# A two-layer graph attention kernel: the range check's PSUM bank, two x tiles turned at other places, and the selection copies on other engines

## The chip, the cores and the metric

The kernel runs on one core of one Trainium2 chip. The metric is the device time of one execution in microseconds (us), the median of several runs. Beside it stands one profiled execution, whose trace gives the start and the duration of every instruction. All times inside the kernel are from the start of that execution's span.

A core has five engines that run their own instruction streams and meet at semaphores: TensorE (PE in the profile; its weight loads are shown apart as PEld), VectorE (DVE), ScalarE (ACT), GpSimd (POOL) and SyncE (SP), which here only issues DMAs. TensorE writes into PSUM, of which this kernel uses eight banks of 128 x 512 fp32.

## The reference

The reference is a two-layer graph attention network with a residual and a layer norm. There are 512 nodes with 768 features and 8192 + 8192 + 512 = 16896 edges (`src`, `dst`), sorted by `dst`.

```python
def gat_layer(x, W, a_s, a_d, b, edge_index, concat):
    h = (x @ W).reshape(n, H, C)
    alpha_s = jnp.einsum('nhc,hc->nh', h, a_s)
    alpha_d = jnp.einsum('nhc,hc->nh', h, a_d)
    e = jax.nn.leaky_relu(alpha_s[src] + alpha_d[dst], NEG_SLOPE)
    m = jax.ops.segment_max(e, dst, num_segments=n)
    e = jnp.exp(e - m[dst])
    denom = jax.ops.segment_sum(e, dst, num_segments=n)
    alpha = e / (denom[dst] + EPS)
    msg = h[src] * alpha[:, :, None]
    out = jax.ops.segment_sum(msg, dst, num_segments=n)
    return out.reshape(n, H * C) + b
h = elu(gat_layer(x, W1, a_src1, a_dst1, b1, ...))     # 8 heads of 768
out = gat_layer(h, W2, a_src2, a_dst2, b2, ...)        # 1 head of 768
return layernorm(x + out)
```

The result depends on the edges only through how often each pair (dst, src) occurs. So the kernel counts the pairs into a 512 x 512 matrix `cnt` and replaces gathers and segment sums by dense matmuls with that matrix.

## The kernel before

**Two passes.** `gat_pass` is traced twice. The first pass (with a `flag`) assumes that each chunk of 128 sorted edges has its destinations in one or two known blocks of 32 nodes. A range check counts how many destinations lie in their block; `flag` is the number of edges minus that count. If it isn't zero, the second, general pass runs; with these inputs it doesn't. All instructions are issued in the order in which the program is written: `manual_schedule` moves nothing, so the order of the source is the order of each engine's stream.

**The loads.** SP issues, in this order: the indices `dst` and `src`, the left halves of W1 for head 0 (two quarters, k chunks 0 to 2 and 3 to 5), x tile 3, the right halves of W1, x tiles 0 and 1, b1, the attention vectors, then the weights of head 1. ScalarE's queue issues x tile 2 at the very start. An x tile is 128 rows of x.

**The opening, lines 148 to 227.** TensorE first runs matmuls on a tile of zeros (`keep_warm`, line 154), whose result in the bank of pool `bc` no one reads. In the meantime GpSimd builds an identity `ident`. From it come the selection columns `pick` (line 212): for each run of chunks with the same blocks, a copy of a few columns of `ident`, repeated once or twice. VectorE makes the runs of the first half of the chunks (16 copies), GpSimd those of the second half (16 copies, between its memsets of `base`, line 215). VectorE converts the indices (`idx_f`, line 217). Two matmuls (line 221) with `pick` and two transposes (line 223) put the indices edge by edge into the PSUM tile `psi`, and VectorE reads it twice: `rel` (line 225), the destination relative to its block, and `idx` (line 227), the sources.

**The x tiles.** `turn_x(t)` (line 353) transposes the six 128 x 128 pieces of an x tile on TensorE (line 357) into two banks of pool `mm`, and ScalarE copies them into `xT` (line 358).

**The counting stage, lines 425 to 528.** There are 132 chunks of 128 edges in nine batches of 16, 16, 13, 16, 13, 16, 13, 16 and 13. For each batch VectorE builds a one-hot of the sources for each chunk (`os`, line 456, 32 rotating buffers) and, in four quarters, one-hots of the destinations (`odw`, line 441). TensorE multiplies the two (line 473, 32 columns of weights), adding into the count tile `cps[t]` of each 128 destinations. Between the counts of two batches the program places pieces ("items") of head 0's projection: an item is three matmuls of line 382 (six rows in the trace, as each fp32 matmul is two), for one x tile, one half of the columns and one half of the contraction. The first items need, in this order, x tile 2 with the first W1 quarter, x tile 2 with the second, then x tile 3 with each. `turns` says before which item another `turn_x` is put. The count of a batch comes after its items. After item 15 come steps of the next head's projection (line 269).

**PSUM.** Pool `mm` has five banks, `tr` two and `bc` one. A tile of a pool takes the pool's banks in rotation, and has to wait until the earlier tile in that bank has been read. In the counting stage `tr` holds, in order, `psi`, `pst`, `cps[0]`, `cps[1]`, `cps[3]` and the tile of `spread(0)`; `bc` holds the warm-up's tile and then `cps[2]`.

**The range check.** `inside` (lines 446 to 450, VectorE, beside batch 0) leaves the number of edges in range per partition in `found`. In batch 1, ahead of the count, TensorE adds the partitions up into `pst` (line 524). In batch 3, ahead of that batch's one-hots, VectorE turns `pst` into `flag` (line 501); in batch 4 the engines load it into registers. `xsums[:1]` (`xS`, line 249), a difference of two parts of `xT` with x tiles 2 and 3, stands behind batch 2's one-hots on VectorE, ahead of the flag.

After the counting stage come, for each of the eight heads, softmax weights, aggregation, and a second projection in a scheme with seven products in place of eight (lines 559 to 918), and at the end the residual with the layer norm.

Of the kernel before, what the change touches and what calls it, by code (L numbers as in the profile page):

```python
# [8 lines left out]
F32 = mybir.dt.float32  # L9
# [14 lines left out]
def kernel(tc: tile.TileContext, *args):  # L24


    with ExitStack() as ctx:
        flags = ctx.enter_context(tc.tile_pool(name="flags", bufs=1))
        ctx.enter_context(tc.manual_schedule())
        flag = flags.tile([1, 1], I32, name="flag")  # L30
        again = gat_pass(tc, flag, *args)
        with tc.If(again != 0):
            gat_pass(tc, None, *args)
# [3 lines left out]
def gat_pass(  # L37
# [16 lines left out]
    nc = tc.nc  # L54
    P = 128
    N, D = x.shape
# [3 lines left out]
    DC = D // P  # L60
    HALF = D // 2
    EC = E // P
    EH = EC // 2
# [7 lines left out]
    keep = ctx.enter_context(tc.tile_pool(name="keep", bufs=1))  # L71
# [6 lines left out]
    mm = ctx.enter_context(tc.tile_pool(name="mm", bufs=5, space=bass.MemoryType.PSUM))  # L78
    tr = ctx.enter_context(tc.tile_pool(name="tr", bufs=2, space=bass.MemoryType.PSUM))
    bc = ctx.enter_context(tc.tile_pool(name="bc", bufs=1, space=bass.MemoryType.PSUM))  # L80
# [52 lines left out]
    x_sb = hpool.tile([P, NT, D], F32, name="hs")  # L133
# [18 lines left out]
    def keep_warm(n):  # L152
        for _ in range(n):
            nc.tensor.matmul(idle, zeros[:, :P], zeros, start=True, stop=True)  # L154

    keep_warm(13)
    nodes = ohp.tile([P, N], F16, name="nodes")
    nc.gpsimd.iota(nodes, pattern=[[1, N]], base=0, channel_multiplier=0,
                   allow_small_or_imprecise_dtypes=True)
    ident = const.tile([P, P], F32, name="ident")  # L160
# [9 lines left out]
                                op=ALU.add)  # L170
    far = const.tile([P, 1], F32, name="far")
    nc.vector.memset(far, -NO_EDGE)


    general = flag is None
    idx_f = ohp.tile([EH, 2, 2, P], F32, name="idx_f")
    if general:
        nc.vector.tensor_copy(idx_f, idx_i)
        idx = ohp.tile([P, 2, EC], F32, name="idx")
        psi = tr.tile([P, 512], F32, name="tr")  # L180
        for j in range(2):
            for r in range(2):
                nc.tensor.transpose(psi[:, (2 * j + r) * EH:(2 * j + r + 1) * EH], idx_f[:, j, r, :],
                                    ident[:EH, :EH])
        nc.vector.tensor_copy(idx, psi[:, :2 * EC].rearrange("p (j c) -> p j c", j=2))
    else:

        B, SLACK = 32, 10  # L190
        blocks = []
        for c in range(EC):
            m = (c + 0.5) * P * N / E
            b = int(m // B)
            lo, hi = b - (m - b * B < SLACK), b + ((b + 1) * B - m < SLACK)
            blocks.append(range(max(lo, 0), min(hi, N // B - 1) + 1))
        at = [0]
        for b in blocks:
            at.append(at[-1] + len(b))
        NB = at[EC]  # L200
        assert NB + EC <= 512 and max(map(len, blocks)) <= 2


        pick = ohp.tile([EH, NB], F32, name="pick")
        base = ohp.tile([P, NB], F32, name="base")
        lo = 0
        while lo < EC:
            hi, k = lo + 1, len(blocks[lo])
            while hi % EH and blocks[hi] == blocks[lo]:
                hi += 1  # L210
            engine = nc.vector if lo < EH else nc.gpsimd
            engine.tensor_copy(pick[:, at[lo]:at[hi]].rearrange("p (c k) -> p c k", k=k),
                               ident[:EH, lo % EH:(hi - 1) % EH + 1].unsqueeze(2).to_broadcast([EH, hi - lo, k]))
            for j, b in enumerate(blocks[lo]):
                nc.gpsimd.memset(base[:, at[lo]:at[hi]].rearrange("p (c k) -> p c k", k=k)[:, :, j], float(b * B))
            lo = hi
        nc.vector.tensor_copy(idx_f, idx_i)
        psi = tr.tile([P, 512], F32, name="tr")
        for r in range(2):
            cols = slice(at[r * EH], at[(r + 1) * EH])  # L220
            nc.tensor.matmul(psi[:, cols], idx_f[:, 0, r, :], pick[:, cols], start=True, stop=True)
        for r in range(2):
            nc.tensor.transpose(psi[:, NB + r * EH:NB + (r + 1) * EH], idx_f[:, 1, r, :], ident[:EH, :EH])
        rel = ohp.tile([P, NB], F16, name="rel")
        nc.vector.tensor_tensor(rel, psi[:, :NB], base, op=ALU.subtract)
        idx = ohp.tile([P, EC], F32, name="idx")
        nc.vector.tensor_copy(idx, psi[:, NB:NB + EC])

    cnt = keep.tile([P, NT, N], F32, name="cnt")
    absent = keep.tile([P, NT, N], BF16, name="absent")  # L230
    xT = keep.tile([P, DC, N], F32, name="xT")
    xS = keep.tile([P, 3, HK, HN], F32, name="xS")
    scr = keep.tile([P, D], BF16, name="scr")
    V = keep.tile([P, DC, 2], F32, name="V")
# [114 lines left out]
            else:  # L349
                nc.sync.dma_start(sums1[name], part)  # L350


    def turn_x(t):
        for ks in (range(4), range(4, DC)):
            ps = mm.tile([P, 512], F32, name="mm")
            for j, k in enumerate(ks):
                nc.tensor.transpose(ps[:, j * P:(j + 1) * P], x_sb[:, t, k * P:(k + 1) * P], ident)  # L357
            nc.scalar.copy(xT[:, ks.start:ks.stop, t * P:(t + 1) * P],  # L358
                           ps[:, :len(ks) * P].rearrange("p (k n) -> p k n", n=P))

    b1T = const.tile([P, H * DC], F32, name="b1T")
    nb1T = const.tile([P, H * DC], F32, name="nb1T")
# [62 lines left out]
    if not general:  # L425
# [53 lines left out]
                done += 1  # L479


        turns = {2: 3, 5: 0, 9: 1}
        keep_warm(1)
        turn_x(2)
        keep_warm(2)
        found = const.tile([P, 1], F32, name="found")
        pst = tr.tile([P, 512], F32, name="tr")
        wholes = len(items)

        extra = {0: [inside], 2: xsums[:1], 4: [lambda: logits(0, HS[0], 2)],  # L490
# [5 lines left out]
        for n, batch in enumerate(batches):  # L496
# [9 lines left out]
            while pos < want:  # L506
                if pos == wholes:
                    pairs = projection(1, XA, B1)
                    items += [lambda p=p: (p[0](), p[1]()) for p in pairs[:4]]
                if pos in turns:  # L510
                    turn_x(turns[pos])
                items[pos]()
                pos += 1
# [15 lines left out]
    else:  # L529
        for t in range(NT):  # L530
            ps = mm.tile([P, 512], F32, name="mm")
            for c in range(EC):
                o1 = ohp.tile([P, P], BF16, name="od", bufs=4)
                o2 = ohp.tile([P, N], BF16, name="os", bufs=32)
                nc.vector.tensor_scalar(o1, nodes[:, t * P:(t + 1) * P], idx[:, 0, c:c + 1], None,
                                        op0=ALU.is_equal)
                nc.vector.tensor_scalar(o2, nodes, idx[:, 1, c:c + 1], None, op0=ALU.is_equal)
                nc.tensor.matmul(ps[:, :N], o1, o2, start=c == 0, stop=c == EC - 1)
            counted(t, ps)
            turn_x(t)  # L540
# [385 lines left out]
    for t in range(NT):  # L926
# [4 lines left out]
        for g, cols in enumerate(parts):  # L931
            ps = mm.tile([P, 512], F32, name="mm")
# [49 lines left out]
```

## Time and profile before

| what | us |
|---|---|
| median of 3 runs | 659.54 |
| lowest and highest run | 658.95, 659.97 |
| the profiled execution's own time | 660.72 |
| its span, first to last instruction | 658.9 |
| busy time of TensorE / VectorE / ScalarE / GpSimd in the span | 646.7 / 508.1 / 248.6 / 51.8 |
| mean granted TensorE clock | 0.994 |

The span in 40 slices of some 16.5 us: each digit is the busy share in tenths, PEclk the granted TensorE clock.

```profile
PE   8899999999999999999999999999999999999995
...
DVE  6998789977779587867779587767776589866785
...
PEclk9899999999999999999999999999999999999998
```

TensorE is busy all through, but for the first two slices and the last. Outside of them VectorE has room. A row such as `25.44 0.83 PE tr L473 x12` in the chain of waits means: from 25.44 us on, for 0.83 us, the chain of work that ended last lay on twelve TensorE instructions of line 473 that write a tile of pool `tr`. In the waits, `PE tr L473 <- DVE flag L501` means that TensorE's instruction of line 473 was held by VectorE's instruction of line 501. A busy time on TensorE is start to modelled end, so a row can be longer than the distance to the next row.

### The profile page before, as it was taken

The page shows a single profiled execution, that of the slowest core. Times are in us where ns is not written, and L with a number is a line of the kernel's source. Part 1 is how long each engine was busy: PE and PEld are TensorE (multiplying, and loading weights), DVE is VectorE, ACT ScalarE, POOL GpSimd, SP SyncE. Part 2 cuts the span into 40 slices and gives each one's busy share as a digit, 9 for nine tenths or more (in the row PEclk, how much of TensorE's full clock was granted, in tenths as well). Part 3 has the DMA queues.
Part 4 walks back from the last instruction along what each step waited for, and adds up shares of the span by engine and source line. Part 5 has one row for each costly group of instructions (what it writes and reads, how often), then busy time and mean ns, then how long its engine had stood idle before and what let it go on. Part 6 is the DMA issues. An engine that isn't in the chain of part 4 may idle for free.

```text
span 658.9 us, 7043 instructions
## 1 busy us (share of the span) xinstructions
PE 646.7 (98%) x2365; PEld 401.0 (61%) x2365; DVE 508.1 (77%) x1116; ACT 248.6 (38%) x417; POOL 51.8 (8%) x106
## 2 busy tenths in 40 slices
PE   8899999999999999999999999999999999999995
PEld 4455577556865577556855577556755545644553
DVE  6998789977779587867779587767776589866785
ACT  2122646350645125350735135530726033333440
POOL 3230011000100110010000110010000100000000
PEclk9899999999999999999999999999999999999998
DMA  8984189177803982087704791197606864000122
GB/s 314 308 143 85 32 258 283 45 218 154 239 0 66 250 227 73 17 236 186 177 1 97 217 258 42 28 253 200 135 1 159 210 210 132 25 0 1 29 59 77
DMA packets 74154, 89.70 MB, mean 136 GB/s; under 512 B 36678, under 2 KB 58750, under 8 KB 74110
## 3 DMA queue, kind: packets, MB, share of 16 engines
q1 hardware_dynamic: 59822, 67.94, 32.8%
q0 software_dynamic: 14000, 20.65, 18.6%
q10 hardware_dynamic: 288, 0.59, 0.3%
q8 instruction: 20, 0.33, 0.2%
q14 instruction: 24, 0.20, 0.1%
HBM read 79.20 MB, written 1.57 MB: 123 GB/s over the span
## 4 chain that ended last, share of the span: by engine, by line
PE 94%; DVE 4%; DMA 0%; ACT 0%; issue 0%; DVEq 0%; ACTq 0%
PE mm L269 60%; PE mm L668 17%; PE mm L614 6%; PE mm L382 4%; PE mm L934 3%; DVE os L456 2%; PE tr L473 1%; PE bc L154 1%; DVE odw L441 1%; PE bc L473 0%; DMA zr<-nr 0%; PE bc L394 0%; PE tr L862 0%; DVE q L571 0%; PE tr L583 0%; PE mm L357 0%
## 5 line engine op out<-in xcount | busy, mean ns | idle before, releaser
L269 PE MATMUL mm<-w,gT 128*128 128x384 f32 x288 | 97.4, 487 | 0.0
L269 PE MATMUL mm<-w,xT 128*128 128x384 f32 x252 | 83.9, 487 | 0.0
L269 PEld LDWEIGHTS mm<-w,gT 128*128 128x128 f32 x288 | 53.9, 190 | 35.7 <-issue 2.0
L269 PEld LDWEIGHTS mm<-w,xT 128*128 128x128 f32 x252 | 47.7, 190 | 33.7 <-PE tr L473 0.4
L269 PE MATMUL mm<-w1t,gS 128*128 128x384 f32 x180 | 60.7, 486 | 0.0
L411 ACT ACTIVATE q<-q,nmax 128x512 f32<-128x512 f32 x36 | 25.8, 722 | 89.9 <-DVE nmax L409 89.9
L269 PE MATMUL mm<-w2t,xS 128*128 128x384 f32 x168 | 56.6, 487 | 0.0
L668 PE MATMUL mm<-PT,hs 128*128 128x256 f32 x216 | 52.6, 379 | 0.0
L672 ACT COPY u<-mm 128x256 f32<-128x256 f32 x18 | 6.7, 372 | 119.2 <-PE mm L668 119.2
L327 DVE TENSOR_TENSOR h<-h,mm 128x384 f32<-128x384 f32 x72 | 39.6, 551 | 14.4 <-PE mm L269 13.8
L269 PEld LDWEIGHTS mm<-w1t,gS 128*128 128x128 f32 x180 | 34.1, 190 | 23.6
L269 PEld LDWEIGHTS mm<-w2t,xS 128*128 128x128 f32 x168 | 31.8, 190 | 22.4 <-issue 0.4
L668 PEld LDWEIGHTS mm<-PT,hs 128*128 128x128 f32 x216 | 41.0, 190 | 7.2 <-issue 0.4
L591 ACT COPY nr<-q 128x1024 uint16<-128x1024 uint16 x32 | 33.4, 1044 | 22.9 <-DVE q L577 16.1
L614 PE MATMUL mm<-PT,hs 128*128 128x512 f32 x96 | 41.6, 593 | 0.0
L596 ACT COPY PT<-zr 128x1024 uint16<-128x1024 uint16 x32 | 37.1, 1160 | 2.0 <-DMA zr<-nr 2.0
L456 DVE TENSOR_SCALAR os<-nodes,idx 128x512 bf16<-128x512 f16 x132 | 35.9, 348 | 1.7 <-PE tr L473 1.7
L668 PE MATMUL mm<-pS,gS 128*128 128x256 f32 x144 | 37.1, 380 | 0.0
L382 PE MATMUL mm<-w,xT 128*128 128x384 f32 x96 | 34.6, 512 | 0.5 <-ACT xT L358 0.5
L104 POOL DMA_DIRECT2D w1t<-in_L_gnn_W_dram x7 | 8.9, 1277 | 315.1 <-PE mm L269 275.7
L269 PE MATMUL mm<-w,gS 128*128 128x384 f32 x96 | 32.6, 486 | 0.0
L269 PE MATMUL mm<-w1t,gT 128*128 128x384 f32 x96 | 32.5, 487 | 0.0
(166 smaller groups left out, 1040.7 us busy)
## 6 DMA issues: line engine op xcount, KB each, us to landing
w<-in_L_gnn_W_dram SPq DMA_DIRECT2D x90, 384.0 KB, 6.3
w<-in_L_gnn_W_dram POOLq DMA_DIRECT2D x15, 576.0 KB, 8.7
w2t<-in_L_gnn_W_dram POOLq DMA_DIRECT2D x13, 576.0 KB, 9.2
w2t<-in_L_gnn_W_dram SPq DMA_DIRECT2D x10, 576.0 KB, 5.0
w1t<-in_L_gnn_W_dram SPq DMA_DIRECT2D x7, 576.0 KB, 4.5
w1t<-in_L_gnn_W_dram POOLq DMA_DIRECT2D x7, 576.0 KB, 8.5
a_s<-in_L_gnn_a_src_dram SPq DMA_DIRECT2D x8, 384.0 KB, 3.7
a_d<-in_L_gnn_a_dst_dram SPq DMA_DIRECT2D x8, 384.0 KB, 3.4
```

What stands on the lines that cost most here:

```text
L104: nc.gpsimd.dma_start(t1, upper[:, :, R], accum_op=ALU.add)
L269: nc.tensor.matmul(ps[:, :HALF], A_[p][:, k, i * P:(i + 1) * P], B_[p][:, k, :], start=start and k == 0, stop=k == HK - 1, skip_group_chec ...
L327: nc.vector.tensor_tensor(a, a, ps, op=ALU.subtract if p == "P7" else ALU.add)
L382: nc.tensor.matmul(ps, xT[:, r * HK + k, t * P:(t + 1) * P], W1[h][r][:, k, cols], start=r == 0 and k == 0, stop=r == 1 and k == HK - 1)
L411: nc.scalar.activation(q, q, AF.Exp, bias=nmax, scale=-1.0)
L456: nc.vector.tensor_scalar(hot[c], nodes, idx[:, c:c + 1], None, op0=ALU.is_equal)
L591: nc.scalar.copy(apart.rearrange("p (h n) -> p h n", h=2), q.bitcast(U16).rearrange("p (n h) -> p h n", h=2))
L596: nc.scalar.copy(PT.rearrange("p s n -> p (s n)").bitcast(U16).rearrange("p (s n h) -> p s n h", s=NT, h=2)[:, :, t * P:(t + 1) * P, :], p ...
L614: nc.tensor.matmul(ps[:, :N], HS[h][:, s, c * P:(c + 1) * P], PT[:, s, :], start=(s == 0), stop=(s == NT - 1))
L668: nc.tensor.matmul(bank[p][:, :HN], A_[p][:, k, c * P:(c + 1) * P], B_[p][:, k, :], start=over is None and k == 0, stop=k == 1, skip_group ...
L672: nc.scalar.copy(u, part("P1"))
L934: nc.tensor.matmul(ps[:, :cols.stop - cols.start], PT[:, s, t * P:(t + 1) * P], h2[:, s, cols], start=(s == 2), stop=(s == 1))
```

## The change

- `pst` is taken from pool `bc` instead of `tr`.
- `turn_x(2)`, x's third tile, moves from the start of the counting stage to just ahead of the index matmuls; for this the definition of `turn_x` and `xT` moves up. The two warm-up matmuls that followed it are gone, and the first warm-up has 9 matmuls instead of 13. One warm-up matmul stays between the index matmuls and the first item.
- `turn_x(3)`, the fourth tile, moves ahead of the second item; it was ahead of the third.
- The selection columns: runs that start below chunk 82 of 132 are copied by VectorE (21 copies), the others by ScalarE (11 copies). GpSimd keeps the memsets of `base`.

Nothing else changes in any engine's stream: the DMAs and their order on all queues are the same, and so are all instructions behind the counting stage.

```diff
-    keep_warm(13)
+    keep_warm(9)
...
+    xT = keep.tile([P, DC, N], F32, name="xT")
+
+
+    def turn_x(t):
+        for ks in (range(4), range(4, DC)):
+            ps = mm.tile([P, 512], F32, name="mm")
+            for j, k in enumerate(ks):
+                nc.tensor.transpose(ps[:, j * P:(j + 1) * P], x_sb[:, t, k * P:(k + 1) * P], ident)
+            nc.scalar.copy(xT[:, ks.start:ks.stop, t * P:(t + 1) * P],
+                           ps[:, :len(ks) * P].rearrange("p (k n) -> p k n", n=P))
...
-            engine = nc.vector if lo < EH else nc.gpsimd
-            engine.tensor_copy(pick[:, at[lo]:at[hi]].rearrange("p (c k) -> p c k", k=k),
-                               ident[:EH, lo % EH:(hi - 1) % EH + 1].unsqueeze(2).to_broadcast([EH, hi - lo, k]))
+            copy = nc.vector.tensor_copy if lo < 5 * EC // 8 else nc.scalar.copy
+            copy(pick[:, at[lo]:at[hi]].rearrange("p (c k) -> p c k", k=k),
+                 ident[:EH, lo % EH:(hi - 1) % EH + 1].unsqueeze(2).to_broadcast([EH, hi - lo, k]))
             for j, b in enumerate(blocks[lo]):
                 nc.gpsimd.memset(base[:, at[lo]:at[hi]].rearrange("p (c k) -> p c k", k=k)[:, :, j], float(b * B))
             lo = hi
         nc.vector.tensor_copy(idx_f, idx_i)
+        turn_x(2)
         psi = tr.tile([P, 512], F32, name="tr")
...
-        turns = {2: 3, 5: 0, 9: 1}
+        turns = {1: 3, 5: 0, 9: 1}
         keep_warm(1)
-        turn_x(2)
-        keep_warm(2)
         found = const.tile([P, 1], F32, name="found")
-        pst = tr.tile([P, 512], F32, name="tr")
+        pst = bc.tile([P, 512], F32, name="bc")
```

## The prediction

> **What bounds the kernel now.** I read the chain of waits first, then the waits of the first 70 us, then the busy time in short windows, then SP's queue. By engine, the chain that ends last reads:
>
> ```profile
> PE 94%; DVE 4%; DMA 0%; ACT 0%; issue 0%; DVEq 0%; ACTq 0%
> ```
>
> So a microsecond taken from TensorE's sequence comes off the span, unless another engine is late behind it. Everything that the change touches lies before 40 us. The chain there, in order of time (start us, us, what):
>
> ```profile
> 1.19 5.54 PE bc L154 x13
> ...
> 7.38 0.38 DVE rel L225
> ...
> 24.46 0.87 DVE xS L249
> 25.32 0.07 DVE flag L501
> 25.40 0.04 issue
> 25.44 0.83 PE tr L473 x12
> 26.27 0.86 PE mm L357 x6
> 27.13 5.51 PE mm L382 x12
> ...
> 34.45 4.07 PE mm L382 x12
> ```
>
> From 7.38 to 25.40 the chain runs through VectorE, and it crosses to TensorE at the flag (line 501), not at a one-hot. The longest waits of that stretch (engine, line, waited for: us, times, longest):
>
> ```profile
> PE tr L473 <- DVE flag L501: 3.1, 1, 3.1
> ...
> DVE os L456 <- PE tr L473: 1.7, 1, 1.7
> ```
>
> The busy time of each engine shows the wait and what follows it (stretch, length, then PE, PEld, DVE, ACT, POOL; granted TensorE clock, DMA share, GB/s):
>
> ```profile
> 22.32:25.44 3.12, 0.00 (x1) 0.00 (x0) 3.12 (x10) 0.00 (x0) 1.28 (x1) 1.00 1.08 348
> 25.44:26.88 1.44, 1.44 (x18) 0.92 (x18) 1.44 (x6) 0.00 (x0) 0.00 (x0) 1.00 1.12 253
> 26.88:30.29 3.41, 3.41 (x8) 1.90 (x7) 3.41 (x12) 0.86 (x2) 0.00 (x0) 0.50 1.14 242
> ```
>
> TensorE stands for 3.12 us, works for 1.44, and is then granted half its clock for 3.41 us. That is why the same twelve matmul rows of line 382 take 5.51 us at 27.13 and 4.07 us at 34.45.
>
> **Why it waits.** Pool tr has two banks: the index transposes take one, pst (the range check) the other, the first count the first again. The second count needs pst's bank, free only when VectorE has read pst for the flag. In VectorE's order that read stands behind batch 2's thirteen one-hots and xS, so it comes at 25.32, although the sum was in PSUM at 21.6.
>
> **The change, part by part.**
>
> *pst in bc's bank.* The second count's bank is now that of the index transposes, read by 7.96. The twelve matmuls of 25.44 follow those that end at 22.32: **3.12 us** off TensorE. The flag still stands in VectorE's order and now holds up bc instead; bc's first count matmul is at 39.50 (about 34.6 after the change), the flag near 25, so some 9.7 us cover it. Without that cover, TensorE would wait in batch 3 as it does now in batch 1.
>
> *The clock behind the gap.* With no gap, the line-382 rows at 27.13 should take 4.07: **1.44 us**. Here row and rule differ. The Trainium skill ("TensorE: Matmul & The Clock Gate", Part 1) puts the clock at half after at least one idle window of about 3.4 us. By that, 3.12 us of standing costs no clock and the sum is 3.5 us. The row shows the loss at 26.88 after a window (23.47 to 26.88, if windows are as long as the 3.41 us at half) with only 1.44 us of work in it. I take the row: the gap paid for the loss.
>
> *x tiles 2 and 3 sooner.* SP's queue gives the landings, since it issues its next load when an earlier one lands:
>
> ```profile
> 2.57 0.48 SPq L141 DMA_DIRECT2D hs<-in_x_dram  x1
> ...
> 8.01 0.34 SPq L129 DMA_DIRECT2D a_s<-in_L_gnn_a_src_dram  x1
> 9.62 0.33 SPq L129 DMA_DIRECT2D a_d<-in_L_gnn_a_dst_dram  x1
> 10.57 0.38 SPq L103 DMA_DIRECT2D w2t<-in_L_gnn_W_dram  x1
> ```
>
> The transfer view says 6.4 us from issue at 1.59 for the first W1 quarter (8.0), 8.0 us from 2.57 for x tile 3 (10.57), 3.8 us from 0.75 for x tile 2 (about 4.6). No DMA instruction moves on any queue. TensorE after the change: nine warm-up matmuls at 0.426 us (5.54/13) end at 5.03; tile 2 is there, six transposes take 0.82 by today's row, up to 1.2 at the half clock (estimate): 5.9 to 6.2; the index matmuls take 0.56 (6.73 to 7.29 now). So VectorE starts line 225 at 6.6 to 6.9 instead of 7.38; I take **0.5 us earlier for VectorE**. Today's first line-382 matmul waits until 8.60 for ScalarE's copy of tile 2; then it starts at W1's landing, 8.05. Three row pairs of 0.68 (4.07/6) reach 10.08; tile 3's transposes, now ahead of the second item, wait for 10.57 (a **new wait of 0.5 us**) and end near 11.5; two items of 2.04 reach 15.6 to 15.7, with ScalarE's copies beside them. The first count starts there instead of 15.98: **0.35 us** off TensorE. Had tile 3 stayed behind the second item, this wait would be nil and today's wait of 0.46 for the copies of tile 3 (at 13.4) would remain: 10.08 + 2.04 + 0.82 + 0.46 + 2.04 = 15.44, so moving tile 3 alone is worth between nothing and a loss of 0.2.
>
> *Six warm-up matmuls fewer, four of them up front.* Nothing by themselves, as the weights land at 8.0. But the same page's closing table asks for at least 4 us of matmuls to release the clock; the nine give 3.84. Row: all thirteen run at 0.426 apiece with 0.63 a row, those after 7.1 at 0.38 a row. So the full rate came between 6.3 and 7.1 and needed most of today's 5.5 us, though the profile prints 1.00 throughout. If the transposes and index matmuls that now fill 5.03 to about 6.9 count as work (Part 4 of the page says transposes don't count alike), nothing is lost. If not, the clock comes a window later, 9.82 or 13.23. To 9.82 the first item ends near 11.0, 0.35 us lost. To 13.23 it ends at 12.12, transposes at 13.3, two items at 17.4: 1.7 us lost. I take 0, as the work on TensorE is unbroken to 6.9, and keep 1.7 for the range.
>
> *Selection copies.* POOL loses sixteen copies of about 0.18 us and is done with its memsets near 3.7 instead of 5.96; no one then waited for it, TensorE being at its warm-up until 6.3. VectorE gets five of them, 0.09 each (1.29/15): 0.43 us inside its 1.41 us wait for the indices before 4.87. ScalarE gets eleven. Nearest row: its 128x48 copy at line 417, 0.20 us with the next started 0.09 later; eleven take 1.1 to 2.2 us after the table load that ends at 2.45, so by 4.7. TensorE needs them at 5.9. Cost nothing; if ScalarE were 2 us later, the one-hots lose about 1 us of the slack below.
>
> **Sum and what is late next.** 3.12 + 1.44 + 0.35 = **4.9 us** on TensorE from 27 us on. VectorE must follow: its one-hots are 0.5 us earlier to batch 3, and its 1.74 us wait at 33.19 for TensorE goes, since the counts that free those buffers end at 29.6 and VectorE arrives at 30.95. So it is 2.24 us earlier from there on. Count starts against the end of their one-hots: batch 0 15.6/13.4, batch 2 27.9/24.0, batch 3 33.6/29.1, batch 7 58.0/56.3, batch 8 63.9/61.6. Smallest margin 1.7 us. Beyond 70 us both kernels have the same instructions in the same order and the chain stays on TensorE, so the shift arrives whole. The profiled execution (span 658.9, own time 660.72) would become 654.0 and 655.8; the median of 659.54, 1.2 below the profiled time, becomes **654.6 us**.
>
> **Rivals.**
> 1. *Late clock.* As above, 0.35 to 1.7 us given back: 655.0 to 656.3, with phase differing by run up to 657. For: four warm-ups fewer and new gaps at 6.9 to 8.0 and 10.1 to 10.6. Against: the unbroken work before. Chance 0.20.
> 2. *VectorE becomes the bound.* Only its own 2.24 us arrive: 657.3. For: it is full from 7.4 to 63.9 but for that one wait. Against: the margins. Chance 0.06.
> 3. *Slower: the clock stays at half.* The first matmuls run cold, and the thin 32-column counts do not release it. Half of the cold time is lost, so it decides against the change once TensorE is cold beyond about 8.05 + 0.5 + 2 x 4.9 = 18.4 us. At 23.5, some two windows more than rival 1, 7.5 us are lost: 662.1. Against: line-382 work at 26.88 recovered in one window. Chance 0.04, with 0.02 for no change.
> 4. *More.* TensorE could gain up to 4.9 + 1.7 = 6.6 before the batch-7 one-hots hold it: 652.9. Chance 0.08.
>
> The forecast, 653.8 to 655.3, has 0.60. A measurement of this kernel tells about 0.2% (1.3 us) from no change. Range 653.2 to 657.3, which holds the forecast, rival 1, the borders of 2 and half of 4. Faster 0.94, within 0.2% 0.02, slower 0.04.
>
> **What would show it.** Right: no wait for the flag at line 473's counterpart; the granted clock 1.00 from 20 to 40 us; first count near 15.6, batch 2's near 27.9; no VectorE wait on TensorE near 31 us; the crossing of chain from VectorE to TensorE gone or before 10 us. Wrong: twelve line-382 rows of over 5 us before 16 us (rival 1), TensorE idle ahead of counts for one-hots (rival 2), index matmuls after 7.4 us (ScalarE's copies or tile 2 late), bc's first count waiting for the flag.

## The result and the profile after

| | before | after |
|---|---|---|
| median of 6 runs, us | 659.38 | 654.92 |
| lowest and highest | 658.91, 660.47 | 654.40, 655.16 |
| ratio, 95% interval | | 0.9929 [0.9917, 0.9942] |
| profiled execution: own time, span | 660.72, 658.9 | 654.95, 653.2 |
| its mean granted TensorE clock | 0.994 | 0.998 |

The change saves 4.5 us in the median; 4.9 were forecast. The two profiled executions differ by more, 5.8 us; why is shown below.

The chain of waits of the changed kernel, by engine:

```profile
PE 95%; DVE 2%; DMA 2%; ACT 0%; SPq 0%; issue 0%; ACTq 0%; DVEq 0%
```

The same chain in order of time (start us, us, what). The line numbers have moved: 473 is now 476, 382 is 385, 524 is 525, and 357 is 181, where `turn_x` stands now.

```profile
2.57 7.65 DMA hs<-in_x_dram
10.22 0.04 issue
10.27 0.87 PE mm L181 x6
11.14 3.87 PE mm L385 x12
15.01 1.41 PE tr L476 x22
16.42 4.07 PE mm L385 x12
20.49 0.09 PE bc L525
20.58 1.34 PE tr L476 x22
21.92 0.81 PE mm L181 x6
22.73 3.87 PE mm L385 x12
```

In this stretch VectorE has left the chain: up to 10.22 us it is the load of x tile 3, and from there on TensorE alone. The second count runs as one piece (20.58); it was two with the gap between them. The range check at 20.49 goes into bc. The rows that took 5.51 us behind the gap take 3.87.

The stretches that held the gap, by busy time (length, then PE, PEld, DVE, ACT, POOL; granted clock, DMA share, GB/s):

```profile
20.00:24.00 4.00, 4.00 (x39) 2.26 (x38) 4.00 (x14) 0.86 (x2) 2.08 (x2) 1.00 1.04 389
24.00:28.00 4.00, 4.00 (x34) 1.98 (x35) 4.00 (x16) 0.79 (x3) 0.41 (x1) 1.00 1.13 256
28.00:32.00 4.00, 4.00 (x19) 2.20 (x12) 4.00 (x10) 1.66 (x3) 1.28 (x1) 1.00 1.10 220
```

TensorE has no gap and the clock stays whole. VectorE is full too. The waits of TensorE's matmuls for loads in the first 70 us, and VectorE's longest wait (engine, line, waited for: us, times, longest):

```profile
DVE q L407 <- ACT q L403: 2.2, 1, 2.2
...
PE mm L385 <- DMA w<-in_L_gnn_W_dram: 0.9, 1, 0.9
...
PE mm L181 <- DMA hs<-in_x_dram: 0.3, 1, 0.3
```

The wait for the flag is gone, and so is VectorE's of 1.7 us on TensorE. New are two short waits for loads, before 8 and before 10.3 us. At 64 us the chain is 6.0 us ahead of before (the last count ends at 64.25 instead of 70.29), and it holds that lead to the last VectorE instruction (647.5 instead of 653.5); 0.3 us go in the last store.

### The profile page after: what moved, and what is told of

Same layout as the page of the kernel before. It is cut to its first block, busy times and chain, and to the rows that moved or that the text cites. A ratio compares the mean times of both kernels' runs of the same rounds, so it can differ in the third digit from the quotient of the medians.

```text
span 653.2 us, 7036 instructions
## 1 busy us (share of the span) xinstructions
PE 643.1 (98%) x2359; PEld 399.7 (61%) x2359; DVE 509.3 (78%) x1121; ACT 250.4 (38%) x428; POOL 50.6 (8%) x90
## 4 chain that ended last, share of the span: by engine, by line
PE 95%; DVE 2%; DMA 2%; ACT 0%; SPq 0%; issue 0%; ACTq 0%; DVEq 0%
PE mm L280 60%; PE mm L669 17%; PE mm L615 6%; PE mm L385 5%; PE mm L935 3%; PE tr L476 1%; DMA hs<-in_x_dram 1%; PE bc L476 0%; DMA zr<-nr 0%; PE bc L397 0%; PE mm L181 0%; PE tr L863 0%; DVE q L572 0%; PE tr L584 0%; DVE q L578 0%
## 5 line engine op out<-in xcount | busy, mean ns | idle before, releaser
L280 PE MATMUL mm<-w,xT 128*128 128x384 f32 x252 | 83.9, 487 | 0.0
L385 PE MATMUL mm<-w,xT 128*128 128x384 f32 x96 | 32.8, 491 | 0.9 <-DMA w<-in_L_gnn_W_dram 0.9
```

The lines of the kernel that those rows point to most:

```text
L280: nc.tensor.matmul(ps[:, :HALF], A_[p][:, k, i * P:(i + 1) * P], B_[p][:, k, :], start=start and k == 0, stop=k == HK - 1, skip_group_chec ...
L385: nc.tensor.matmul(ps, xT[:, r * HK + k, t * P:(t + 1) * P], W1[h][r][:, k, cols], start=r == 0 and k == 0, stop=r == 1 and k == HK - 1)
```

## The experiments

Each was timed beside fresh runs of the kernel before on the same chip, in three series. Differences are of medians, in us against those runs unless another kernel is named; ratios have the 95% interval.

| run | median | before beside it | ratio to before |
|---|---|---|---|
| before again | 659.86 | 659.55 | 1.0004 [0.9995, 1.0013] |
| bank only | 655.71 | 659.55 | 0.9945 [0.9932, 0.9959] |
| change without the bank | 659.14 | 659.55 | 0.9996 [0.9985, 1.0008] |
| gap filled with matmuls | 658.45 | 659.55 | 0.9987 [0.9978, 0.9996] |
| flag read early | 655.32 | 659.66 | 0.9937 [0.9923, 0.9950] |
| after again | 654.74 | 660.20 | 0.9927 [0.9910, 0.9943] |
| after, 13 warm-ups | 655.22 | 660.20 | 0.9931 [0.9915, 0.9947] |
| after, 2 warm-ups | 656.22 | 660.20 | 0.9951 [0.9935, 0.9966] |
| after, tile 3 later | 656.61 | 660.20 | 0.9948 [0.9930, 0.9966] |
| the same, standing time filled | 655.46 | 659.66 | 0.9940 [0.9926, 0.9953] |
| after, copies on GpSimd | 654.98 | 659.66 | 0.9928 [0.9914, 0.9941] |
| after, tile 3 loaded first | 654.22 | 659.66 | 0.9919 [0.9905, 0.9932] |

The median of before itself moves, with the share of its runs that show the lower granted clock of 0.993 or 0.994: 13 of 27, 8 of 11 and 6 of 9 in the three series. So a difference to before carries some 0.5 us of this into any comparison across series.

### The kernel before, once more

No edit.

> The kernel before, unchanged, for its spread and its clock. Theory A (the sum of the prediction): 0 us; the trace shows again the 3.1 us wait for the flag and then about 3.4 us at half the clock, 1.4 to 1.7 us lost. Rival: the half clock depends on where the 3.4 us windows fall in a run, so this trace shows less or none of it, and the profiled execution of before (660.72, 1.3 above the median) was one with much of it.

The trace shows the wait (3.0 us) and a stretch of half clock again. It begins sooner (near 25.4, where the first trace had 26.88), so it covers the transposes too: they take 1.47 us and the twelve rows at 26.93 take 4.86, where the first trace had 0.86 and 5.51. Together the loss is the same. The 27 runs of before in that series fall into two groups by their mean granted clock: 13 at 0.993 or 0.994 with a median of 659.85, and 14 at 0.996 to 0.998 with a median of 658.8. So about half of these runs of before lose the clock, and in the median those are some 1 us longer; the profiled execution of 660.72, at 0.994, belonged to them. The rival is right in that the loss depends on the run.

### The bank alone

```diff
-        pst = tr.tile([P, 512], F32, name="tr")
+        pst = bc.tile([P, 512], F32, name="bc")
```

> Before with pst in bc's bank alone. Theory A: the wait of 3.1 us and the clock loss behind it go, 4.6 to 5 us in the trace and 3.1 to 5 in the median, first count still at 16 us. Rival, VectorE is the bound: only its own 1.7 us wait goes, 1.7 us. Rival, the opening carries the gain: under 1 us.

3.8 us faster (655.71 against 659.55). Its chain has `21.93 1.34 PE tr L473 x22` and `24.08 3.87 PE mm L382 x12`: no gap, no half clock. The first count starts at 16.30, so nothing came from the opening. The one changed word carries some four fifths of the gain; the two rivals, at most 1.7 us, fall.

### The change without the bank

```diff
-        pst = bc.tile([P, 512], F32, name="bc")
+        pst = tr.tile([P, 512], F32, name="tr")
```

> After with pst back in tr: only the opening is changed. Theory A: the chain still crosses from VectorE to TensorE at the flag, and VectorE comes 0.5 to 0.8 us earlier to it, so 0.5 to 0.8 us faster than before, with a flag wait of 3.1 + 1.0 - 0.6 = about 3.5 us on TensorE. Rival, the opening carries the gain: 2 us or more. Rival, the half clock: no gain or slower.

0.4 us faster, which the interval doesn't tell from nothing. The wait for the flag stands in its trace (engine, line, waited for: us, times, longest):

```profile
PE tr L476 <- DVE flag L502: 3.9, 1, 3.9
```

It is longer than the 3.5 expected. TensorE came sooner to it, and the end of the wait is set by VectorE, whose `rel` began at 7.50 in this execution, no earlier than before. As long as the flag holds TensorE, a faster opening of TensorE only lengthens the wait. The longer wait can cost more clock, too, which the rival named. This execution (661.65) and one other (661.56) lie some 2 us above the other nine runs, and its chain runs at half rate through all three rows behind the gap, which take 0.80, 0.81 and 3.87 us when the gap is filled (next section):

```profile
25.06 1.47 PE tr L476 x11
26.53 1.47 PE mm L181 x6
28.00 5.42 PE mm L385 x12
```

The clock is halved there from about 24.2 to 31.0 us, twice as long as in the traces of before.

### The gap filled

Twelve warm-up matmuls stand ahead of line 473's first matmul into the second count's bank; the flag still holds that bank.

```diff
                     if t not in cps:
+                        if t == 1:
+                            keep_warm(12)
```

> Before with twelve warm-up matmuls (2.6 us) ahead of the first matmul of the second count, so that TensorE works in the gap and the wait for the flag stays. Theory A (the gap pays for the half clock): the twelve rows behind it take about 4 us instead of 5.5, so 1.4 to 1.7 us less in the trace, less in the median if not every run of before lost the clock. Rival (the clock is lost for another reason): 0 us and the half clock stays. Rival (the fill itself delays): slower by up to 0.5 us.

1.1 us faster, with all eleven runs at a clock of 0.996 or more. Its chain in order of time:

```profile
21.19 0.69 PE tr L475 x10
21.88 2.70 PE bc L154 x12
24.58 0.80 PE tr L475 x12
25.38 0.81 PE mm L357 x6
26.19 3.87 PE mm L382 x12
```

The second count still waits for its bank: the flag is written at 24.50 (24.36 + 0.14), and the fill, from 21.88 to 24.58, ends 0.1 us later. But the twelve rows behind it take 3.87 us. So standing still costs twice, once as time and once as clock; the second part is worth 1.1 us in the median.

### The flag read early

The bank stays in tr; VectorE reads the sum behind batch 2's first one-hot, instead of behind all thirteen and xS. (This is the place that the expectation calls "behind the first one-hot of the second wave's neighbour".)

```diff
-            if n == 3:
-                nc.vector.tensor_scalar(flag, pst[:1, :1], -1.0, float(E), op0=ALU.mult, op1=ALU.add)
-            hot = {c: o for wave in batch for c, o in sources(wave).items()}
+            hot = {}
+            for i, wave in enumerate(batch):
+                if n == 2 and i == 1:
+                    nc.vector.tensor_scalar(flag, pst[:1, :1], -1.0, float(E), op0=ALU.mult, op1=ALU.add)
+                hot.update(sources(wave))
```

> Before with VectorE's flag read put behind the first one-hot of the second wave's neighbour, near 21.5 us, instead of behind batch 2 and xS; pst stays in tr. Theory A (the wait came from the place of the read in VectorE's order, not from the bank as such): TensorE waits under 0.3 us, no half clock behind it, 3 to 4.5 us faster than before, like the bank alone (655.7). Rival, the bank itself is what costs: under 1 us. Rival, VectorE now waits for the sum and the one-hots come late: slower than the bank alone by more than 0.5 us.

4.3 us faster (655.32 against 659.66), as good as the bank. VectorE's instructions in order of time show what it pays (start, us, engine, line, what; in brackets the idle time before and its releaser):

```profile
19.71 0.35 DVE L456 TENSOR_SCALAR os<-nodes,idx 128x512 bf16<-128x512 f16 x1
21.11 0.14 DVE L503 TENSOR_SCALAR flag<-tr 1x1 int32<-1x1 f32 x1 [1.06 <-PE tr L526]
21.18 2.06 DVE L456 TENSOR_SCALAR os<-nodes,idx 128x512 bf16<-128x512 f16 x7
```

VectorE now waits 1.06 us for the sum, and that costs nothing, as its one-hots are early enough. TensorE goes through: `21.05 1.34 PE tr L473 x22`. So it was the place of the read in VectorE's order that held the bank, and either end of the wait can be moved.

### After, once more, with thirteen and with two warm-up matmuls

```diff
-    keep_warm(9)
+    keep_warm(13)
```

> The changed kernel, unchanged, as the base of the three beside it: 654.9 us, 0.7% below before, first count at about 15 us.

> After with 13 warm-up matmuls up front. Theory A (the nine cost nothing, but four more delay the work behind them by up to 4 x 0.43 = 1.7 us, most of it inside the wait for the weights to 7.7 us): first count 0.2 to 0.6 us later, median 0.2 to 0.6 us above after. Rival, the late clock: with nine the half clock reaches into the first items, so thirteen are faster than after by 0.3 to 1.7 us.

After again gives 654.74. With thirteen it is 655.22, in the range expected, but the intervals overlap. In its trace the warm-ups aren't the reason: the thirteen were done by 5.7, the index matmuls began at 6.16 (after again: 6.06), and the first count is late (15.81 against 15.55) because x tile 3 landed at 11.09 instead of 10.83. Inconclusive as to a cost; no gain from more warm-up is seen.

The other direction has `keep_warm(2)` in the same place.

> After with 2 warm-up matmuls up front (3 us of work less before the weights land). Theory A (transposes and index matmuls count as work and the wait for x tile 3 covers a late clock): within 0.4 us of after. Rival, the late clock: the first items of line 382's kind run at half rate, 0.35 us lost if the clock comes near 9.8, 1.7 if near 13.2; the first count at 15.3 to 16.7 instead of 14.9.

656.22, that is 1.5 us above after again. The chain:

```profile
8.16 3.56 PE mm L385 x6
11.73 0.65 PE mm L181 x6
12.38 3.87 PE mm L385 x12
```

The first six rows take 3.56 us; six rows at full rate take 1.94 (the run with tile 3 loaded first, below), so 1.6 us less. At full rate they would have ended near 10.1 and tile 3 landed at 10.59, so the wait for it hides some 0.5 of that. The late clock, a rival of the prediction, is a real mechanism, at about its forecast price. Nine warm-ups kept it out of these rows in every trace of after, two did not.

### Tile 3 later, and the same with the standing time filled

```diff
-        turns = {1: 3, 5: 0, 9: 1}
+        turns = {2: 3, 5: 0, 9: 1}
```

> After with x tile 3 turned where before had it, ahead of the third item. Theory A (tile 3 alone is worth between nothing and a loss of 0.2): the wait of 0.3 to 0.5 for the landing goes, a wait of 0.46 for ScalarE's copies comes back, within 0.3 us of after. Rival: turning it sooner is what the opening's gain of 0.8 us rests on, so this is slower than after by 0.5 us or more.

656.61, and not as expected. The six runs are 655.11, 655.24 and 656.11 at a clock of 0.996 or 0.997, and 657.11, 657.26 and 657.45 at 0.993 or 0.994. The profiled one is of the latter (stretches by busy time, as above):

```profile
5.00:8.30 3.30, 1.71 (x15) 1.40 (x14) 2.27 (x4) 0.86 (x2) 0.00 (x0) 1.00 1.00 358
8.30:11.70 3.40, 3.40 (x6) 1.80 (x6) 3.40 (x13) 0.00 (x0) 0.00 (x0) 0.50 1.07 386
```

TensorE was done with the opening at 6.55 and stood 1.59 us until W1's first quarter landed. Then it was granted half the clock for 3.4 us, over rows that were on the chain: twelve took 5.82 us. The Trainium skill ("TensorE: Matmul & The Clock Gate", Part 1) says the windows run free of the program, so where they fall differs from run to run; the two groups of runs fit that.

Filling the standing time, with tile 3 still later:

```diff
-        keep_warm(1)
+        keep_warm(5)
```

> After with x tile 3 turned ahead of the third item, and with four more warm-up matmuls behind the index matmuls, where TensorE stands until W1 lands. Theory B (with the tile later, half of the runs lost 1.7 us because standing from 6.5 to 8.1 us halved the clock for one window): no run of over 656 us, median 655.0 to 655.6, within 0.5 us of after. Rival (the order of tile 3 itself cost those 1.5 us): 656 to 657 again, with twelve rows of line 385 near 4.1 us and yet a late first count.

655.46, no run above 655.92, and the stretch is whole:

```profile
5.00:8.30 3.30, 3.30 (x21) 2.44 (x20) 1.89 (x4) 0.86 (x2) 0.00 (x0) 1.00 0.96 336
8.30:11.70 3.40, 3.40 (x13) 2.02 (x12) 3.40 (x12) 0.01 (x1) 0.00 (x0) 1.00 1.06 390
```

So the clock was most of what the slower three runs lost: they lie 2.0 us above the other three, and with the standing time filled no run is like them. What is left is small. From the start of the first item to the first count this trace needs 7.28 us (7.62 to 14.90); after needs 7.14 (7.80 to 14.94), and after again the same: turning tile 3 sooner is worth 0.14 us on this way. In the median the filled run is 0.5 us above the one with the copies on GpSimd, of the same series and with after's TensorE stream, but their runs overlap. One thing stays open. After has the same TensorE stream up to W1's landing, so it should be as exposed to the half clock there. In after again TensorE stood there for 1.42 us and kept the clock, and none of after's eleven timed runs, nor of the five with the copies on GpSimd, has a clock below 0.996. Three of six runs against none of sixteen makes mere chance unlikely, but no run shows what else would make the difference.

### The copies back on GpSimd

```diff
-            copy = nc.vector.tensor_copy if lo < 5 * EC // 8 else nc.scalar.copy
+            copy = nc.vector.tensor_copy if lo < EH else nc.gpsimd.tensor_copy
```

> After with the second half of the selection copies back on GpSimd. Theory A (they cost nothing where they stood): GpSimd is done near 6.0 us, when TensorE comes to the index matmuls at 5.9 to 6.1, so at most 0.2 us on VectorE, which is not the bound; the median equals after's within 0.3 us. Rival, the copies held the opening: VectorE's line 237 starts 0.5 us later and the median is 0.5 us or more above after.

654.98, the same as after. GpSimd's last memset begins at 5.79, before the index matmuls (6.29). Line 237 does start late in this trace, at 7.49 instead of 6.81, as the rival has it; but here TensorE's transposes ahead of the index matmuls took 1.28 us instead of 0.99, so the delay isn't shown to be the copies', and the median doesn't move. This part of the change does nothing that can be measured.

### Tile 3's load first

In after, the first count hangs on the landing of x tile 3. This puts its load ahead of W1's second quarter, and has the four warm-up matmuls in the standing time.

```diff
         for r in range(2):
             nc.sync.dma_start(W1[0][r][:, :, cols], ...)
-        for t in tiles:
-            nc.sync.dma_start(x_sb[:, t, :], x[t * P:(t + 1) * P, :])
+            for t in tiles:
+                if (t == 3) == (r == 0):
+                    nc.sync.dma_start(x_sb[:, t, :], x[t * P:(t + 1) * P, :])
...
-        keep_warm(1)
+        keep_warm(5)
```

> After with x tile 3's load issued ahead of W1's second quarter instead of behind it, and the same four warm-up matmuls more. Theory A (after the change the first count hangs on the landing of x tile 3 at 10.2 to 10.8): the tile lands 1 to 1.5 us earlier, inside the first item, the second quarter later, near 10.5; the first count 0.3 to 0.5 us earlier, the median 0 to 0.5 us below after. Rival (the second quarter becomes the wait): no gain, up to 0.3 us slower.

654.22, the lowest of all, 5.4 us under before. It is 0.5 to 0.8 us under the medians of after and of the copies on GpSimd, at or above the upper end of what was expected, but the runs overlap. Two things differ from after, the order of the loads and the fill, and the gain isn't divided between them. The chain has no wait for a load:

```profile
7.53 1.94 PE mm L386 x6
9.46 0.66 PE mm L182 x6
10.12 3.87 PE mm L386 x12
13.99 1.41 PE tr L477 x22
```

First item to first count is 6.56 us (7.36 to 13.92) against 7.14.

## Why the prediction was right, point by point

- **What bounds the kernel, and the wait for the flag (3.12 us).** Right. The bank alone and the early read, two edits that share only the end of this wait, bring 3.8 and 4.3 us. Taking off 1.1 us for the clock leaves 2.7 and 3.2 us for the wait in the median. The cover for the flag was there as well: it is read at 24.48, and bc's first count starts at 33.3.
- **The clock behind the gap (1.44 us, the row taken over the rule).** The mechanism is right: a gap of under 3.4 us did cost the clock, and filling it brought the clock back. In the profiled pair the term is 1.64 us (5.51 to 3.87). In the median it is about 1.1, since not every run of before loses it (13 of 27 in that series). This term was mis-sized: the sum was made against one execution and carried whole to the median. The 1.2 us by which that execution stood above the median were taken for a constant; the profiled execution of after stands 0.03 above its own. If the windows are 3.41 us long, as the prediction took them, the one ahead of the half clock held 1.44 us of TensorE work in the first trace of before, 0.8 in the second, and 1.8 in the opening of the run with tile 3 later: the clock went after windows up to about half full.
- **The opening (0.35 us).** Right in sign for TensorE, and perhaps too small. In the profiled pair the first count started at 14.94 instead of 15.98. Of that 1.04 us, 0.33 is x tile 3 landing earlier in this execution (10.24 for 10.57), so the pair flatters it. Over five traces with the opening of before the first count starts at 15.24 to 16.30, 15.7 in the mean; over four with that of after (after twice, without the bank, copies on GpSimd) at 14.82 to 15.55, 15.1 in the mean. In medians the opening is what parts after from the two kernels that mend the gap alone: 0.8 us to the bank alone, in another series, and 0.3 from the early read (655.32) to the copies on GpSimd (654.98) in one series.
- **VectorE 0.5 us earlier.** Not shown. In the profiled pair its line 225 (now 237) starts at 6.81 instead of 7.38, but over the same traces it starts at 6.62 to 7.69 with the old opening and at 6.81 to 7.50 with the new one, 7.1 and 7.2 in the mean: how long the warm-ups and transposes take in an execution moves it by more than the change does.
- **The sum (4.9 us) and the median (4.5).** The gap with its clock brought less in the median, 3.8 and 4.3 for 4.56; the opening brought 0.3 to 0.8 for 0.35. That the forecast is so close is in part luck, as an error of the one kind made up for the other.
- **The new wait for tile 3's landing (0.5).** Right in kind, 0.3 us in both traces of after, ahead of 10.27 and 10.88.
- **Moving tile 3 alone, between nothing and a loss of 0.2.** Wrong in sign. From the first item to the first count the sum had 7.55 us with tile 3 moved and 7.39 without; the traces have 7.14 and 7.28. The moved order was overpriced, the wait at 0.5 instead of 0.3 us and the two items behind it at 4.08 instead of 3.87. Apart from that the kernel without the move lost 1.9 us in the median, mostly by the clock: the sum took TensorE's standing before W1's landing as free and left out that the clock is decided there too. Why after, with the same standing, doesn't lose it isn't shown.
- **Nine warm-up matmuls cost nothing.** Right as far as seen: thirteen bring nothing. Rival 1 had its price right, and shows at two. (Rival 3's 23.5 us lies three windows of 3.41 us behind rival 1's 13.23, not two; its loss of 7.5 us is summed from 23.5 and stands.)
- **The selection copies cost nothing.** Right; undone, they change nothing either.
- **VectorE is not late.** Right. Batch 4's one-hots start at 30.62 (30.95 forecast) with no wait, and no count of after waits for one. But it is closer than forecast: batch 7's one-hots are done at 56.07 and its count starts at 56.86, 0.8 us of margin instead of 1.7, as TensorE came more forward in this execution than the sum said.

## What to carry to other kernels

A PSUM bank is held until its last reader has run, and the reader's place in its own engine's order decides when: for a small result that nobody is in a hurry for, look at who needs the bank next. A gap on TensorE is priced here as its length (3.1 us) plus the clock behind it (1.6 us in a trace that loses it), and the second part differs by run, so a sum made from one profiled execution needs the granted clock of the other runs beside it before it is carried to a median. Standing time that no work can fill may still be worth filling with dummy matmuls (1.1 us here).

## What the runs showed that was not expected

TensorE ran at half rate in the opening while the profile printed a granted clock of 1.00: with two warm-ups, six rows of line 385 took 3.56 us in a stretch (8 to 11 us) printed as 1.00. The rate has to be read from the durations there. The time at which the full rate came also differs between executions of the same opening: the thirteen warm-ups up front hold the chain for 4.47 us in one of the five executions with before's opening, and for 4.79, 5.10, 5.54 and 5.73 us in the others, and the index work follows them.
